# Two products of a 4-bit weight decode: one VectorE operation or two on GpSimd, in a kernel whose order of work is planned

## The chip, the cores and the metric

The kernel runs on one core of a Trainium2 chip. The metric is the device time of one execution in microseconds (us), the median of several. The engines of a core work side by side, each through its own queue of instructions in order: TensorE (PE in the profile, its weight loads PEld), VectorE (DVE), ScalarE (ACT), GpSimd (POOL) and SyncE (SP), which here only issues DMA transfers. An instruction waits on semaphores for what it needs, and everything behind it in its queue waits with it.

## The reference

A layer adds two branches to its input `x` of 8 sequences x 256 tokens x 256 features, both from the same normalized input.

- Attention branch, 16 heads of 128: `q`, `k`, `v` and a gate by weights of 256 x 2048; `q` and `k` are turned by position (rope). A low-rank product gives 64 states per head and token, `s`; `es = exp(s)` and `z` is the running log-sum-exp of `s` over the tokens. `ok = exp(-z) * (masked(q k^T) @ es)`, a softmax over the 64 states, then `W2 = masked((softmax * exp(-z)) @ es^T)`, `o = W2 @ v`, an RMS norm, the gate, and a product with `Wo`.
- Feed-forward branch of width 2048 whose three weight matrices are stored as 4-bit codes with one scale for each block of 32:

```python
idx = jnp.stack([W_packed & 15, W_packed >> 4 & 15], axis=-1).reshape(N, -1)
vals = NVFP4_LUT[idx]              # 0, 0.5, 1, 1.5, 2, 3, 4, 6 and their negatives
W = vals.reshape(N, K // 32, 32) * scales[:, :, None]
...
gelu = tanh(0.79788 * (gate + 0.044715 * gate ** 3)) * gate * 0.5 + gate * 0.5
out = (gelu * up) @ Wd.T
```

All of it is fp32.

## The kernel before

**Tiles.** The 2048 tokens are worked in 4 groups of 512. A step `n` is one group and one pair of heads: 4 x 8 = 32 steps, with a step -1 ahead that prepares step 0, and a last one that finishes. For a step, PE does `rope` four times (Q and K of two heads, L645), `states` (L584), `value` and `gate` (`vg`, L706), `scores` for each head (L725, L728), `logits` (L745), `cross` (L820), `weights` (L845, with `apply`, L872), `outputs` for each head (L888) and, every second step, `close` (L941), the product with `Wo`. Between these, units of the feed-forward branch are fed: `ffn_gate` (L437), `ffn_up` (L466) and `ffn_down` (L491): for each quarter of the width and each token group four gate and up pairs, then two down projections.

**Who does what around them.** For a rope, ScalarE copies the swapped halves of the PSUM result (`z`, L655 and L656), VectorE multiplies by the cosine (L658), and GpSimd multiplies `z` by the sine (L663) and adds (L664). The scores are masked by VectorE (L716). `states` is clipped (L598), turned to `u` and `es` by ScalarE and a transpose through DRAM (L602, L519, L523, L532, L612), summed along the tokens by a VectorE scan (L624) and inverted (L630). The softmax takes row maxima on VectorE (L781, L786) and exponentials on ScalarE (L792); GpSimd multiplies the result by `enz` (L803). `outputs` ends in a power on GpSimd (L910), for which VectorE's product (L914) waits. The norm of later groups is on VectorE (L290 to L306) and ScalarE (L309). A gate unit uses ScalarE, GpSimd (L446) and VectorE (L448, L452), an up unit VectorE (L475).

**The decode.** 24 parts (4 quarters, each with two halves of gate, up and down) are decoded into `w_gate`, `w_up` and `w_down` by `decode_next`. For one part VectorE shifts the codes so that a 4-bit code's fields land in sign, exponent and mantissa of an fp32 number (L388, twice), masks them (L392), and multiplies by a power of two and by the scales (L394). The buffer `u` has two copies and is shared with `states`; `pk` (codes) and `sc` (scales) have three, and SP loads the next when their last reader is done.

**The order.** Each engine's queue is written out by the program itself while it is built, and kept as written (`tc.manual_schedule()`). PE's units are placed at fractions of a step by the tables `POS`, `START`, `NORM_AT`, and feed-forward units are spread by `FEED`, `FIRST` and `LAST`; `DUE` says how many parts have been decoded by which step. The work of the other engines is written as chains: a generator yields an engine and an assumed cost ("v" VectorE, "s" ScalarE, "g" GpSimd, "d" DMA issue) ahead of each operation, and `advance` always writes out the chain that could begin first by assumed clocks (then by `rank`; the decode has the lowest). A changed cost or place so moves other operations in the queues, too.

Of the kernel before, what the change touches and what calls it, by code (L numbers as in the profile page):

```python
# [10 lines left out]
F32 = mybir.dt.float32  # L11
I32 = mybir.dt.int32
AF = mybir.ActivationFunctionType
ALU = mybir.AluOpType
# [3 lines left out]
P = 128  # L18
# [15 lines left out]


POS = {'scores': (0.054, 0.064),
 'logits': (0.12,),
 'softmax': (0.335,),
 'cross': (0.147,),
 'weights': (0.169,),  # L40
 'low': (0.121,),
 'states': (0.167,),
 'outputs': (0.364, 0.453),
 'close': (0.384, 0.559),
 'rope': (0.176, 0.315, 0.368, 0.485),
 'vg': (0.561, 0.79, 0.922, 0.953)}
START = {-1: {'states': (0.575,), 'rope': (0.155, 0.358, 0.421, 0.588)},
 0: {'vg': (0, 0.013, 0.059, 0.197),
     'scores': (0.082, 0.162),
     'states': (0.336,),  # L50
     'logits': (0.251,),
     'softmax': (0.433,),
     'rope': (0.211, 0.24, 0.245, 0.458)}}
FEED = {-1: (0.336, 1.0)}
NORMS = {0: 1, 2: 2, 5: 3}
WO = (1, 3, 4, 6)
NORM_AT = (0.204, 0.657)
FIRST = [0.27, 1.57]
LAST = [1.65, 3.53]
DUE = [4, 6, 7, 7, 9, 9, 10, 11, 11, 11, 12, 13, 14, 15, 16, 16, 16, 17, 18, 19, 19, 22, 23, 23, 24]  # L60


@with_exitstack
def layer_kernel(ctx: ExitStack, tc: tile.TileContext, a: dict, out: bass.AP):
# [15 lines left out]
    nc = tc.nc  # L80
# [84 lines left out]
    def new(pool, shape, tag, bufs=1, dtype=F32):  # L165

        users = held.setdefault(tag, [])
        if len(users) >= bufs:
            while any(c in chains for c in users[-bufs]):
                advance()  # L170
            floor[0] = max([floor[0]] + [c.at for c in users[-bufs]])
        t = pool.tile(shape, dtype, tag=tag, name=tag, bufs=bufs)
        users.append([])
        at_tag[id(t)] = t, users[-1]
        return t
# [8 lines left out]
    def chain(gen, *tiles, rank=1, at=0.0):  # L184


        c = Chain()
        c.rank = rank
        c.banks = []
        c.gen, c.at, c.what = gen, max(clock["pe"] + 0.2, floor[0], at), next(gen)  # L190
        floor[0] = 0.0
        chains.append(c)
        for t in tiles:
            users = at_tag[id(t)][1]
            users.append(c)
            if id(t) in banks_taken:
                c.banks.append(users)
        return c
# [155 lines left out]
    LD, CH = 512, 256  # L354
# [3 lines left out]
    def load_packed(m):  # L358

        if m < 12:  # L360
            pk = new(de, [P, LD], "pk", 3, I32)
            sc = new(de, [P, LD], "sc", 3)
            nc.sync.dma_start(out=pk, in_=a["codes"][m])
            nc.sync.dma_start(out=sc, in_=a["scales"][m])
            packed[m] = pk, sc
            loads(m, 512)

    def decode_next():

        q, k = divmod(len(parts), 6)
        m, o = 3 * q + (0, 1, 0, 1, 2, 2)[k], (0, 0, CH, CH, 0, CH)[k]
        if k == 1 and q:
            load_packed(m + 1)
        if k >= 4:
            load_packed(3 * q + k - 1)
        w = (w_gate, w_up, w_down)[m % 3]
        pks, scs = packed[m]
        pk, sc = pks[:, o : o + CH], scs[:, o : o + CH]  # L380
        f = q * LD + o if m % 3 == 2 else o // CH * (MLP // 2) + q * CH
        w = w[:, :, f : f + CH]
        u = new(de, [P, 2, CH], "u", 2, I32)

        def work():
            yield "v", 0.6
            for k, left in enumerate((28, 24)):
                nc.vector.tensor_scalar(  # L388
                    u[:, k, :], pk, left, 6, ALU.logical_shift_left, ALU.arith_shift_right
                )  # L390
            yield "v", 1.4
            nc.vector.tensor_scalar(u, u, 0x81C00000 - (1 << 32), None, ALU.bitwise_and)  # L392

            nc.vector.scalar_tensor_tensor(  # L394
                w, u.bitcast(F32), 2.0 ** (125 if m % 3 == 2 else 126),
                sc.unsqueeze(1).to_broadcast([P, 2, CH]), ALU.mult, ALU.mult,
            )

        parts.append(chain(work(), pks, scs, u, rank=2, at=landed[m]))

    inter = {}
# [96 lines left out]
    def ffn():  # L498

        for q in range(4):  # L500
            for g in range(NG):
                for n in blocks(q):
                    yield ffn_gate, g, n
                    yield ffn_up, g, n
                for i in (0, 2):
                    yield ffn_down, g, q, i
# [464 lines left out]
    banks = NG * (MLP // P * 2 + 8)  # L971
    weight = FIRST + [1.0] * (N + 2 - len(FIRST) - len(LAST)) + LAST
    feeding = list(ffn())
# [29 lines left out]
    for n in range(-1, N + 1):  # L1003
        at = []
        pos = START.get(n, {})

# [4 lines left out]
        def put_at(place, f, *args):  # L1011
            at.append((place, len(at), f, args))

        def put_norm(g, places):
            for k, h in enumerate((0, 2)):
                put_at(places[k], norm, g, h)
# [24 lines left out]
        if gn:  # L1041
            if gn > 1:
                put_at(0.0, load_x, gn * TC, TC)
            put_norm(gn, NORM_AT)
        if n > 0:
# [10 lines left out]
        upto = round(banks * sum(weight[: n + 2]) / sum(weight))  # L1056
        lo, hi = FEED.get(n, (0.0, 1.0))
        for k in range(upto - fed):
            put_at(lo + (hi - lo) * (k + 0.5) / (upto - fed), feed)
        fed = upto  # L1060
        upto = DUE[n + 1] if n + 1 < len(DUE) else 24
        for k in range(sent, upto):
# [93 lines left out]
```

## Time and profile before

| | |
|---|---|
| median of 3 runs | 1188.27 us (1187.34 to 1188.94) |
| the profiled execution, its own time | 1187.13 us |
| its span in the profile | 1185.3 us |
| granted TensorE clock | 1.00 |
| ScalarE busy | 536.3 us (45%) |
| DMA, mean | 114 GB/s |
| HBM read and written | 88.47 MB, 45.61 MB |

The span runs from the first instruction's start to the last one's end. "Busy" is the union of an engine's instructions; idle time is put down to what released the next instruction. PE's matmuls are pipelined and their ends modelled, so where PE lost time is read from the start of a matmul after a gap. Rows of groups have the form: line, engine, operation, out<-in, shapes, count | busy us, mean ns of one | idle us of the engine ahead of them, and what ended it. All lines in the text are those of the kernel before; in the changed kernel those after the decode stand 3 lower.

### The profile page before, as it was taken

How to read it: one execution, taken by the hardware profiler on the slowest of the kernel's cores; microseconds unless marked ns; L12 is line 12 of the kernel's file. 1: busy time of each engine (PE TensorE's matmuls, PEld its weight loads, DVE VectorE, ACT ScalarE, POOL GpSimd, SP SyncE). 2: the span in 40 equal slices, each digit the busy share in tenths (PEclk: the TensorE clock that was granted, in tenths of full speed). 3: DMA queues.
4: the chain of work that ended last, by engine and by line, in shares of the span. 5: the costliest groups of instructions: out<-in, count | busy, mean ns of one | idle time of the engine just before them, and what ended most of it. 6: DMA issues, size and time to landing. Idle time of an engine off the chain costs nothing.

```text
span 1185.3 us, 18158 instructions
## 1 busy us (share of the span) xinstructions
PE 1171.9 (99%) x5830; PEld 827.7 (70%) x5830; DVE 884.7 (75%) x1690; ACT 536.3 (45%) x1685; POOL 494.1 (42%) x439
## 2 busy tenths in 40 slices
PE   9899999999999999999999999999999999999998
PEld 6466776866767777667767677686776777766775
DVE  7978968887677788767587875968778577768553
ACT  3545535455344444443354543435544444445321
POOL 5434525554344444434344442434544334445110
PEclk9999999999999999999999999999999999999999
DMA  6335444453333342333344243434333333432321
GB/s 209 116 105 153 143 118 152 132 144 116 101 119 117 110 140 84 107 113 107 90 142 123 86 121 107 120 103 122 96 97 96 116 116 107 124 102 88 98 64 61
DMA packets 143087, 135.30 MB, mean 114 GB/s; under 512 B 21264, under 2 KB 110480, under 8 KB 142992
## 3 DMA queue, kind: packets, MB, share of 16 engines
q1 hardware_dynamic: 142992, 134.15, 38.5%
q8 instruction: 46, 0.75, 0.3%
q14 instruction: 49, 0.40, 0.1%
HBM read 88.47 MB, written 45.61 MB: 113 GB/s over the span
## 4 chain that ended last, share of the span: by engine, by line
PE 89%; DVE 6%; DMA 2%; issue 1%; POOL 1%; ACT 1%; SPq 1%; DVEq 0%; ACTq 0%; POOLq 0%
PE ps L645 17%; PE ps L706 17%; PE ps L491 9%; PE ps L941 9%; PE ps L437 8%; PE ps L466 8%; PE ps L888 5%; PE ps L725 4%; PE ps L745 3%; PE ps L845 3%; PE ps L728 2%; PE ps L584 2%; PE ps L872 1%; PE ps L820 1%; DVE enz L630 1%
## 5 line engine op out<-in xcount | busy, mean ns | idle before, releaser
L663 POOL TENSOR_TENSOR z<-z,turns 128x512 f32<-128x512 f32 x128 | 169.4, 1324 | 209.3 <-ACT z L656 209.0
L645 PE MATMUL ps<-xT,wts 128*128 128x512 f32 x512 | 239.2, 599 | 0.5 <-ACT xT L349 0.5
L706 PE MATMUL ps<-wts,xT 128*128 128x256 f32 x1024 | 235.7, 379 | 1.5 <-DVE og L914 1.1
L706 PEld LDWEIGHTS ps<-wts,xT 128*128 128x128 f32 x1024 | 194.4, 190 | 54.1 <-issue 24.4
L645 PEld LDWEIGHTS ps<-xT,wts 128*128 128x128 f32 x512 | 90.1, 190 | 82.0 <-issue 75.1
L446 POOL TENSOR_SCALAR t<-t 128x512 f32<-128x512 f32 x64 | 40.2, 629 | 196.6 <-ACT t L444 194.6
L437 PE MATMUL ps<-xT,w_gate 128*128 128x512 f32 x256 | 120.7, 594 | 0.1
L466 PE MATMUL ps<-xT,w_up 128*128 128x512 f32 x256 | 120.6, 594 | 0.0
L630 DVE RECIPROCAL enz<-enz 128x128 f32<-128x128 f32 x128 | 117.6, 932 | 0.0
L491 PE MATMUL ps<-w_down,inter 128*128 128x256 f32 x512 | 115.3, 380 | 0.0
L941 PE MATMUL ps<-w_o,ogT 128*128 128x256 f32 x496 | 112.1, 379 | 0.0
L941 PEld LDWEIGHTS ps<-w_o,ogT 128*128 128x128 f32 x496 | 94.1, 190 | 24.7 <-issue 12.4
L491 PEld LDWEIGHTS ps<-w_down,inter 128*128 128x128 f32 x512 | 96.6, 190 | 15.9 <-issue 3.2
L655 ACT COPY z<-ps 64x512 f32<-64x512 f32 x128 | 74.5, 582 | 69.8 <-PE ps L645 60.3
L444 ACT ACTIVATE t<-ps 128x512 f32<-128x512 f32 x64 | 38.2, 596 | 137.9 <-PE ps L437 137.8
L910 POOL TENSOR_TENSOR ss<-ss,nhalf 128x4 f32<-128x4 f32 x64 | 66.0, 1032 | 69.7 <-DVE ss L906 68.4
L409 DVE TENSOR_TENSOR res<-ps,res 128x512 f32<-128x512 f32 x63 | 42.9, 681 | 69.5 <-PE ps L491 48.0
L664 POOL TENSOR_TENSOR k<-k,z 128x512 f32<-128x512 f32 x64 | 83.7, 1308 | 26.5 <-DVE k L658 16.7
L664 POOL TENSOR_TENSOR q<-q,z 128x512 f32<-128x512 f32 x64 | 85.0, 1328 | 21.2 <-DVE q L658 17.2
L803 POOL TENSOR_TENSOR prT<-okT,enz 128x512 f32<-128x512 f32 x32 | 40.8, 1274 | 119.9 <-DMA okT<-by_way 106.6
L792 ACT ACTIVATE ok<-okT,mx 128x64 f32<-128x64 f32 x256 | 85.7, 339 | 10.8 <-DVE mx L786 10.3
L448 DVE TENSOR_TENSOR t<-ps,t 128x512 f32<-128x512 f32 x64 | 43.7, 684 | 60.9 <-POOL t L446 60.7
(83 smaller groups left out, 1936.6 us busy)
## 6 DMA issues: line engine op xcount, KB each, us to landing
wts<-in_wqkvg_dram SPq DMA_DIRECT2D x64, 512.0 KB, 3.8
by_way<-ok SPq DMA_DIRECT2D x256, 64.0 KB, 1.8
okT<-by_way SPq DMA_DIRECT2D x64, 256.0 KB, 2.7
by_way<-og SPq DMA_DIRECT2D x256, 64.0 KB, 1.8
ogT<-by_way SPq DMA_DIRECT2D x64, 256.0 KB, 2.9
by_way<-u SPq DMA_DIRECT2D x128, 64.0 KB, 1.8
u<-by_way SPq DMA_DIRECT2D x32, 256.0 KB, 2.8
pk<-in_codes_dram SPq DMA_DIRECT2D x12, 256.0 KB, 3.1
```

Source lines behind the costliest of these rows:

```text
L437: nc.tensor.matmul(pg, lhsT=w_gate[:, c, ns], rhs=xT[:, c, gs], start=c == 0, stop=c == 1)
L466: nc.tensor.matmul(pu, lhsT=w_up[:, c, ns], rhs=xT[:, c, gs], start=c == 0, stop=c == 1)
L491: nc.tensor.matmul(ps[:, k, :], lhsT=inter[g, n][0][:, (i + k) * P : (i + k + 1) * P], rhs=w_dn[:, n, :], start=n == 2 * q, stop=n == 2 * ...
L630: nc.vector.reciprocal(r, r)
L645: nc.tensor.matmul(ps, lhsT=w[:, c, :], rhs=xT[:, c, g * G : (g + 1) * G], start=c == 0, stop=c == 1)
L655: nc.scalar.copy(z[0:64], pv[64:128])
L663: nc.gpsimd.tensor_tensor(z, z, sin_b, ALU.mult)
L664: nc.gpsimd.tensor_tensor(y, y, z, ALU.add)
L706: nc.tensor.matmul(ps[:, k, :], lhsT=xT[:, c, tt], rhs=w[:, which, c, :], start=c == 0, stop=c == 1,)
L792: nc.scalar.activation(pr[:, js, i, :], okT[:, js, i, :], AF.Exp, bias=mx[:, k : k + 1], scale=SCALE, accum_out=sm[:, k : k + 1],)
L910: nc.gpsimd.tensor_tensor(ss, ss, nhalf, ALU.pow)
L941: nc.tensor.matmul(ps[:, k, :], lhsT=ogT[hh][0][:, i + k], rhs=w_o[:, (hp // 2) * 4 + hh, :], start=hh == 0, stop=hh == 3,)
```

## The change

The cost assumed for L392 is 0.5 us by itself; the two products become two GpSimd operations with an assumed cost of 1.95 us: first by the power of two, from `u` into the weight tile, then by the scales in place. The tables of places and the number of decoded parts by step are set anew.

```diff
 POS = {'scores': (0.054, 0.064),
- 'logits': (0.12,),
+ 'logits': (0.148,),
...
- 'low': (0.121,),
+ 'low': (0.116,),
...
- 'close': (0.384, 0.559),
- 'rope': (0.176, 0.315, 0.368, 0.485),
+ 'close': (0.372, 0.61),
+ 'rope': (0.176, 0.368, 0.375, 0.523),
...
-START = {-1: {'states': (0.575,), 'rope': (0.155, 0.358, 0.421, 0.588)},
- 0: {'vg': (0, 0.013, 0.059, 0.197),
+START = {-1: {'states': (0.575,), 'rope': (0.155, 0.358, 0.421, 0.592)},
+ 0: {'vg': (0.044, 0.057, 0.103, 0.241),
...
-     'rope': (0.211, 0.24, 0.245, 0.458)}}
-FEED = {-1: (0.336, 1.0)}
+     'rope': (0.238, 0.267, 0.272, 0.485)}}
+FEED = {-1: (0.443, 1.0)}
...
-NORM_AT = (0.204, 0.657)
-FIRST = [0.27, 1.57]
-LAST = [1.65, 3.53]
-DUE = [4, 6, 7, 7, 9, 9, 10, 11, 11, 11, 12, 13, 14, 15, 16, 16, 16, 17, 18, 19, 19, 22, 23, 23, 24]
+NORM_AT = (0.204, 0.593)
+FIRST = [0.17, 1.57]
+LAST = [1.56, 3.5]
+DUE = [4, 6, 7, 7, 8, 9, 11, 11, 11, 11, 12, 13, 14, 15, 16, 16, 16, 16, 18, 19, 19, 22, 23, 23, 24]
...
-            yield "v", 1.4
+            yield "v", 0.5
             nc.vector.tensor_scalar(u, u, 0x81C00000 - (1 << 32), None, ALU.bitwise_and)
-
-            nc.vector.scalar_tensor_tensor(
-                w, u.bitcast(F32), 2.0 ** (125 if m % 3 == 2 else 126),
-                sc.unsqueeze(1).to_broadcast([P, 2, CH]), ALU.mult, ALU.mult,
+            yield "g", 1.95
+
+            nc.gpsimd.tensor_scalar(
+                w, u.bitcast(F32), 2.0 ** (125 if m % 3 == 2 else 126), None, ALU.mult
+            )
+            nc.gpsimd.tensor_tensor(
+                w, w, sc.unsqueeze(1).to_broadcast([P, 2, CH]), ALU.mult
             )
```

## The prediction

> **What bounds the kernel now.** I read the busy times first, then a table of stretches, then who waited for whom before 62 us, and last the timeline where TensorE (PE) waits. Busy times:
>
> ```profile
> PE 1171.9 (99%) x5830; PEld 827.7 (70%) x5830; DVE 884.7 (75%) x1690; ACT 536.3 (45%) x1685; POOL 494.1 (42%) x439
> ```
>
> PE lacks 13.4 us in a span of 1185.3, and no change to other engines can give back more. Where they lie (stretch, then its length, then PE, PEld, DVE, ACT, POOL busy):
>
> ```profile
> 0.00:10.00 10.00, 7.90 (x40) 6.65 (x41) 3.98 (x15) 2.58 (x5) 3.07 (x13) 1.00 0.72 229
> 20.00:40.00 20.00, 19.12 (x74) 12.50 (x75) 19.75 (x34) 8.33 (x15) 10.21 (x9) 1.00 0.30 98
> 40.00:60.00 20.00, 16.05 (x67) 8.62 (x64) 19.72 (x43) 11.27 (x31) 10.47 (x10) 1.00 0.50 146
> 60.00:200.00 140.00, 138.20 (x682) 96.11 (x679) 114.04 (x218) 67.16 (x211) 64.46 (x57) 1.00 0.48 140
> 200.00:1100.00 900.00, 898.76 (x4562) 640.59 (x4560) 677.75 (x1291) 420.95 (x1343) 388.56 (x334) 1.00 0.38 111
> 1100.00:1186.00 86.00, 81.89 (x386) 58.97 (x384) 41.12 (x80) 20.64 (x71) 11.48 (x14) 1.00 0.23 72
> ```
>
> 2.1 us are lost before the first work and 4.1 at the end (0.7 of that is the table's 1186.0 against the span's 1185.3); nothing in the diff reaches the loads and the last output that cause most of these. Between 200 and 1100 us PE lacks 1.2 us in 900. What can move is 20 to 60 us, 4.8 us, where VectorE (DVE) is busy 39.5 of 40, and 60 to 200 us, 1.8. The operations that the edit touches or copies:
>
> ```profile
> L394 DVE SCALAR_TENSOR_TENSOR w_gate<-u,sc 128x512 f32<-128x512 f32 x8 | 8.7, 1083 | 0.3
> L394 DVE SCALAR_TENSOR_TENSOR w_up<-u,sc 128x512 f32<-128x512 f32 x8 | 7.4, 930 | 0.3
> L394 DVE SCALAR_TENSOR_TENSOR w_down<-u,sc 128x512 f32<-128x512 f32 x8 | 6.5, 811 | 0.3
> L446 POOL TENSOR_SCALAR t<-t 128x512 f32<-128x512 f32 x64 | 40.2, 629 | 196.6 <-ACT t L444 194.6 <-DVE eps L798 0.4
> L803 POOL TENSOR_TENSOR prT<-okT,enz 128x512 f32<-128x512 f32 x32 | 40.8, 1274 | 119.9 <-DMA okT<-by_way 106.6 <-PE ps L728 10.8 <-PE ps L820 2.3
> ```
>
> The longest PE stall of the run, in the timeline (start, length, engine, line):
>
> ```profile
> 51.03 0.58 ACT L655 COPY z<-ps 64x512 f32<-64x512 f32 x1
> 51.62 0.58 ACT L656 COPY z<-ps 64x512 f32<-64x512 f32 x1
> 52.63 0.62 ACT L309 ACTIVATE z<-res,off,rstd 128x256 f32<-128x256 f32 x1 [0.43 <-DVE off L306]
> 53.15 0.33 ACT L792 ACTIVATE ok<-okT,mx 128x64 f32<-128x64 f32 x1
> 53.23 1.27 POOL L663 TENSOR_TENSOR z<-z,turns 128x512 f32<-128x512 f32 x1
> 54.68 1.27 POOL L664 TENSOR_TENSOR k<-k,z 128x512 f32<-128x512 f32 x1 [0.18 <-DVE k L658]
> 56.01 0.70 PE L725 MATMUL ps<-q,k 128*128 128x256 f32 x2 [2.61 <-POOL k L664]
> ```
>
> The scores of step 1's second head need K, and K needs ScalarE's two copies (L655, L656), then two GpSimd products (L663, L664). The copies were done at 52.20, before the norm (L309) and the softmax exponentials (L792). Soon after, PE waits 1.34 and 0.19 us more for VectorE's L716; its first down projection (L491) starts at 61.79.
>
> **The change part by part.** *Removed:* 24 operations, 8 x 1083 + 8 x 930 + 8 x 811 = 22.6 us of VectorE. The shortest is 0.69 us, so 16.6 us are work and 6.0 are waiting: at 12.57 one took 1.64 while GpSimd's L663 ran from 12.36 to 13.66.
>
> *Added:* 24 x (0.63 by L446 + 1.27 by L803) = 45.6 us of GpSimd, 494 to 540 us, 46% of the span: no bound. [...] More GpSimd time also holds up VectorE's other two-SBUF operations; against 22.6 us of relief at 75% load I cost this at nothing after 60 us. Cover gone, it is the 6.0 us above scaled by 45.6/494, 0.6 us.
>
> *Moved, up to 60 us.* START and FEED only change the sequence of PE's first units, not their number: at 37 us both orders have done the same ones. I read the built order of each queue and laid rows of the same shape along it. Six of the 24 decodes lie here. On GpSimd the first now stands ahead of the first rope: 12.6 + 0.63 + 1.27 = 14.5, where L663 started at 12.36. The second stands between the third and fourth rope, ready about 25.8, while the first up projection is reached at 24.5: PE waits 1.3. In exchange the two waits of before at 29.24 and 30.65 (0.40 and 0.48 idle) shrink, since VectorE loses six products of 1.64, 1.64, 0.98, 0.69, 0.69 and 0.69 = 6.3 us. PE is then some 1 us late, which the next stall swallows.
>
> *That stall grows.* rope's new places (0.368, 0.375, 0.523 for 0.315, 0.368, 0.485) and the planner's new costs put ScalarE's two copies for this K behind both norm operations, all eight exponentials and the copy of es (L612). In the old trace that group runs from 52.63 to 56.91, 4.3 us. It can't start before the row maxima (L786). Logits come earlier, about 37 for 39.4, but on VectorE the maxima now stand behind two scans (L624) and a K product, which meet GpSimd at two decodes on end. I take the start as 53.15, as before, give or take 1. Copies then run from 57.4 to 58.6, the two GpSimd products to 61.2; L725 starts at 61.2 (60.2 to 62.2) for 56.01, 5.2 later. Behind K's product on VectorE, ahead of the last L716, stand L658, two L452, two L475, L392 and two L716: 0.68 + 1.36 + 1.38 + 0.43 + 1.1 = 5.0 from 58.6 to 63.6. PE, after scores (1.3) and cross (0.5), is ready at 63.0: 0.6 idle for 1.53. Net at the first down projection: 5.2 - 0.9 = +4.3, with bounds +2.4 and +5.9.
>
> *After 62 us.* 18 decodes remain, 1.9 us of GpSimd each. In seven the next GpSimd instruction is the power L910, for which VectorE's L914 waits, with all behind it. Bounds: -1.8 (all idle between 60 and 200 us gone; logits moved from 0.12 to 0.148 give L716 1 us more) and 7 x 1.9 = +13.3 (nothing hidden). The nearest row is the 1.2 us that PE lacks in 900 us with GpSimd 43% busy, so near the lower end: +1.0. The decodes end about 850 us; the last step's order on PE is the same, so the end (FIRST, LAST, close) costs nothing; without that cover, a wait like the 0.33 us of L888 at 1145.71. Norms, DUE and SP: the load of the third scales waits on SP for GpSimd's product (about 32 us) instead of VectorE's (24.1), with the next weights behind it; those are needed near 75 us, so nothing.
>
> *Sum.* The profiled execution took 1187.13, 1.83 above its span, and 1.14 under the median. 1187.13 + 4.3 + 1.0 = 1192.4; with 1.1 to the median, 1193.5. Bounds: 1188.3 + 2.4 - 1.8 = 1188.9 and 1188.3 + 5.9 + 4 = 1198.2 (4: two of the seven places unhidden).
>
> **The rivals.** *Faster (0.16).* VectorE is what PE waits for until 60 us; it loses 6.3 us there, the exponentials start early enough (before 49 us) for the copies to be no later than before, and the idle time of 0.40, 0.48, 1.34, 0.19 and 2.61 goes: 5.0 us, 1183.3. For it: DVE's 39.5 of 40. Against: the order on ScalarE. It decides if K's copies end before 52.2.
>
> *No change (0.14).* PE stays at 99% with all of it hidden: K late by 2 us, the later waits less by 2: 1188.3. For it: 1.2 us idle in 900.
>
> *GpSimd's queue becomes the chain after 62 us (0.12).* More than two of the seven powers reach PE: 4.3 + 13.3, 1205.9 at most, about 1202. Against it: VectorE's idle quarter.
>
> That the change does less than it says is excluded: all 24 pairs stand in GpSimd's built order.
>
> **How the numbers follow.** Forecast 0.58 (1188.9 to 1198.2). With 0.12 for the third rival, whose time is above the forecast, slower by over 0.2% has 0.70; 0.2% (2.4 us) is about what a measurement of this kernel can tell from no change. The range, 1185.0 to 1201.0, leaves out most of the fast case and the top of the third rival.
>
> **What the profile would show.** Right: L394 gone, 24 pairs on POOL of 0.63 and 1.3 us; VectorE near 860 us; the longest PE stall before L725 near 55 to 61 us, put to GpSimd's K, with ScalarE's copies directly after L612; first L491 near 66. Wrong: that L725 starts by 57 us, PE idle before 60 us under 5 us, or PE idle between 200 and 1100 us over 5.

## The result, and the profile after

The change makes the kernel slower by 0.3%: 1191.79 us (1189.97 to 1193.48, 9 runs) against 1187.69 us (1187.15 to 1188.94, 9 runs) of the kernel before on the same chip, a ratio of 1.0029 with an interval of 1.0020 to 1.0038. That is 4.1 us, where 5.3 were forecast. The profiled execution took 1191.79 us, with a span of 1189.6, 4.3 us more than before. Busy times after:

```profile
PE 1173.1 (99%) x5830; PEld 828.9 (70%) x5830; DVE 872.0 (73%) x1666; ACT 537.7 (45%) x1685; POOL 557.1 (47%) x487
```

VectorE lost 12.7 us and GpSimd gained 63.0; the forecast had 22.6 and 45.6. The table of stretches (start and end, length, then PE, PEld, DVE, ACT, POOL, the granted clock, DMA share, GB/s) shows where PE stands still now:

```profile
20.00:40.00 20.00, 18.44 (x81) 12.45 (x80) 19.44 (x34) 8.53 (x16) 15.79 (x14) 1.00 0.35 106
40.00:60.00 20.00, 14.16 (x40) 6.44 (x38) 17.16 (x38) 11.48 (x31) 14.05 (x13) 0.92 0.47 134
60.00:200.00 140.00, 137.94 (x686) 97.97 (x687) 109.61 (x215) 65.99 (x209) 75.84 (x66) 0.97 0.49 135
200.00:1100.00 900.00, 899.38 (x4561) 639.18 (x4560) 674.19 (x1277) 422.24 (x1343) 428.02 (x363) 1.00 0.39 112
```

From 20 to 60 us PE lacks 1.56 + 5.84 = 7.4 us where it lacked 4.8. In the 900 us after 200 it lacks 0.6, half of what it lacked before. The clock column is new: it is below 1.00 in two rows. The timeline around the longest stall (start, length, engine, line; what ended the wait in brackets):

```profile
51.88 0.35 ACT L795 ACTIVATE ok<-okT,mx 128x64 f32<-128x64 f32 x1 [0.37 <-DMA wts<-in_wqkvg_dram]
...
56.43 0.60 ACT L615 COPY es<-u 128x512 f32<-128x512 f32 x1
...
57.06 0.58 ACT L658 COPY z<-ps 64x512 f32<-64x512 f32 x1
57.66 0.58 ACT L659 COPY z<-ps 64x512 f32<-64x512 f32 x1
...
58.74 1.27 POOL L666 TENSOR_TENSOR z<-z,turns 128x512 f32<-128x512 f32 x1 [3.48 <-ACT z L659]
...
60.19 1.27 POOL L667 TENSOR_TENSOR k<-k,z 128x512 f32<-128x512 f32 x1 [0.18 <-DVE k L661]
...
61.51 1.22 PE L728 MATMUL ps<-q,k 128*128 128x256 f32 x2 [6.73 <-POOL k L667]
```

ScalarE's copies for K stand directly behind the copy of `es`, and the scores start at 61.51 us. The first of these products took 1.22 us; the same one took 0.70 at 53.21. Four windows of the same table, a few microseconds long, show the granted clock at that time (the third number from the right):

```profile
54.00:58.00 4.00, 0.79 (x6) 0.54 (x4) 4.00 (x10) 3.88 (x13) 1.17 (x2) 0.87 0.01 3
58.00:62.00 4.00, 0.49 (x1) 0.49 (x2) 4.00 (x9) 1.38 (x3) 2.54 (x2) 0.50 0.30 80
...
64.00:66.00 2.00, 2.00 (x15) 1.53 (x15) 0.56 (x1) 0.37 (x1) 1.92 (x3) 0.50 0.67 180
66.00:68.00 2.00, 2.00 (x16) 1.40 (x13) 0.26 (x1) 0.00 (x0) 0.92 (x1) 0.71 0.37 80
```

While PE stood still its granted clock fell to 0.50. It was back at 1.00 only at about 67.2 us (a mean of 0.71 over 2 us is 1.2 us at a half), 5.7 us after work resumed. If a half clock does half the work, an estimate (the product above took 1.22 us for 0.70), those 5.7 us cost 2.8.

At the end of the run PE waits once more, for the last softmax but one (`prT`):

```profile
1112.75 1.16 PE L848 MATMUL ps<-prT,esT 64*128 64x128 f32 x16 [1.23 <-POOL prT L806]
```

The last group that matters is that of the new products:

```profile
L395 POOL TENSOR_SCALAR w_up<-u 128x512 f32<-128x512 f32 x8 | 12.8, 1601 | 11.5 <-DVE u L392 11.0 <-DVE eps L801 0.4
...
L395 POOL TENSOR_SCALAR w_gate<-u 128x512 f32<-128x512 f32 x8 | 12.0, 1497 | 6.1 <-DVE u L392 4.9 <-DVE ss L909 1.1
...
L398 POOL TENSOR_TENSOR w_down<-w_down,sc 128x512 f32<-128x512 f32 x8 | 10.2, 1274 | 0.7
...
L449 POOL TENSOR_SCALAR t<-t 128x512 f32<-128x512 f32 x64 | 40.0, 624 | 143.6 <-ACT t L447 140.9
```

The second product (L398) costs the 1.27 us that L803 had shown. The first (L395) costs 1.5 to 1.6 us, where L449, an operation of the same kind, shape and engine, costs 0.62.

### The profile page after: what moved, and what is told of

Read it like the earlier page. It is cut to its first block, busy times and chain, and to the rows that moved or that the text cites. A ratio compares the mean times of both kernels' runs of the same rounds, so it can differ in the third digit from the quotient of the medians.

```text
span 1189.6 us, 18152 instructions
## 1 busy us (share of the span) xinstructions
PE 1173.1 (99%) x5830; PEld 828.9 (70%) x5830; DVE 872.0 (73%) x1666; ACT 537.7 (45%) x1685; POOL 557.1 (47%) x487
## 4 chain that ended last, share of the span: by engine, by line
PE 91%; POOL 3%; DMA 2%; DVE 2%; issue 1%; ACT 1%; SPq 0%; POOLq 0%; DVEq 0%; ACTq 0%
PE ps L648 18%; PE ps L709 17%; PE ps L944 9%; PE ps L494 9%; PE ps L440 8%; PE ps L469 8%; PE ps L891 5%; PE ps L728 4%; PE ps L748 3%; PE ps L848 2%; PE ps L731 2%; PE ps L587 2%; PE ps L823 2%; PE ps L875 1%; DMA okT<-by_way 1%
## 5 line engine op out<-in xcount | busy, mean ns | idle before, releaser
L449 POOL TENSOR_SCALAR t<-t 128x512 f32<-128x512 f32 x64 | 40.0, 624 | 143.6 <-ACT t L447 140.9
L891 PEld LDWEIGHTS ps<-v,wt 128*128 128x128 f32 x512 | 66.0, 191 | 28.6 <-issue 13.9
L728 PE MATMUL ps<-q,k 128*128 128x256 f32 x256 | 77.7, 385 | 7.7 <-POOL k L667 7.7
```

What stands on the lines that cost most here:

```text
L728: nc.tensor.matmul(ps[:, 0:T], lhsT=k[:, b, 0:P], rhs=q[:, b, :], start=True, stop=True)
L891: nc.tensor.matmul(po[:, i, :], lhsT=wt[:, i, :], rhs=v[:, i, j * DK : (j + 1) * DK], start=False, stop=i == TC - 1,)
```

## The experiments

Two theories at the start. *A:* the new order costs the time, through the stall at K. *B:* the operation costs it, because its GpSimd time holds somebody up. Unless said otherwise each edit is against the changed kernel, times are medians, and the ratio is to the kernel before, measured beside it (1187.7 to 1188.1 us). Times inside a profile are those of one execution; executions of one kernel lie 1 to 7 us apart, so differences of under a microsecond between two profiles are a hint only.

**The order alone** (`e1_order_only`): the new tables and assumed costs, with VectorE's one operation where the pair stood.

```diff
-            nc.gpsimd.tensor_scalar(
-                w, u.bitcast(F32), 2.0 ** (125 if m % 3 == 2 else 126), None, ALU.mult
-            )
-            nc.gpsimd.tensor_tensor(
-                w, w, sc.unsqueeze(1).to_broadcast([P, 2, CH]), ALU.mult
+            nc.vector.scalar_tensor_tensor(
+                w, u.bitcast(F32), 2.0 ** (125 if m % 3 == 2 else 126),
+                sc.unsqueeze(1).to_broadcast([P, 2, CH]), ALU.mult, ALU.mult,
             )
```

> The changed kernel's queues on every engine as they are, but each decode's products are again one VectorE operation, where its pair of GpSimd operations stood in the order. Theory A (the new order costs the time: on ScalarE the two copies for K of step 1's second head stand behind the softmax exponentials): the scores of that head still start at 60 to 62 us, the first down projection at 65.5 to 68 (67.62 in the changed kernel, 61.79 before), and the time is 1190 to 1192. Theory B (the GpSimd operations cost it: 1.5 and 1.27 us each ahead of the ropes): the scores start by 57, the first down projection by 63, and the time is 1187 to 1188.5.

1188.35 us, 1.0002 (0.9993 to 1.0011). The stall is there all the same: the scores of the second head wait 6.6 us and start at 60.56, and the first down projection starts at 65.85, as A expected; the time is the one that B expected. The end of the span comes 0.2 us after that of before. Starts of the same units in three profiles, with the delay to before:

| start of | before | after | order alone |
|---|---|---|---|
| first down projection | 61.79 | 67.62 (+5.83) | 65.85 (+4.06) |
| scores, step 4 | 163.71 | 167.15 (+3.44) | 164.92 (+1.21) |
| scores, step 8 | 300.94 | 304.75 (+3.81) | 301.94 (+1.00) |
| scores, step 28 | 1000.41 | 1002.98 (+2.57) | 1000.24 (-0.17) |
| scores, step 31 | 1100.21 | 1102.38 (+2.17) | 1099.64 (-0.57) |
| end of the span | 1185.35 | 1189.64 (+4.29) | 1185.59 (+0.24) |

The new order loses 4 us at K and has it back by the end: waits that before had after 62 us, such as 1.06 us at 119.63 and 0.40 at 128.66, are gone. From 60 to 1100 us PE lacks 1.3 us here and 3.0 before; the difference is less than half of what comes back, and where the rest lies was not found. (Feed-forward units that moved between steps are part of the single rows, not of the last one.) Theory A falls. What is left, 4.05 us of span, is the operation in this order: 1.8 by the first down projection, 1.0 more by step 28, 1.3 in the last steps. Of the 1.8, 0.95 is K's later arrival (scores at 61.51 for 60.56) and 0.8 is, by the estimate above, a longer time at half clock after it (5.7 us for 4.0).

**The operation alone** (`e2_op_only`): the tables and assumed costs of before, with the GpSimd pair.

```diff
-            nc.vector.scalar_tensor_tensor(
-                w, u.bitcast(F32), 2.0 ** (125 if m % 3 == 2 else 126),
-                sc.unsqueeze(1).to_broadcast([P, 2, CH]), ALU.mult, ALU.mult,
+            nc.gpsimd.tensor_scalar(
+                w, u.bitcast(F32), 2.0 ** (125 if m % 3 == 2 else 126), None, ALU.mult
+            )
+            nc.gpsimd.tensor_tensor(
+                w, w, sc.unsqueeze(1).to_broadcast([P, 2, CH]), ALU.mult
             )
```

(against the kernel before)

> The kernel before with its places, its assumed costs and so its queues, only that each decode's single VectorE product is the pair of GpSimd operations. Theory A: the scores of step 1's second head start within 1.5 us of 56.0, the first down projection within 2 of 61.79, no down-clocking, and the time is 1187 to 1189.5, the small loss from the first gate or up projection that waits for its weights. Theory B: 1191 or more, with the first down projection later than 65.

1206.8 us, 1.0156 (1.0142 to 1.0170). In the list of waits (for whom; total us, times, longest) K's GpSimd product leads:

```profile
PE ps L727 <- POOL k L666: 14.6, 5, 5.9
```

Without new places the operation costs 18.7 us; the tables take back 15 of them. So one part of the change is a repair of the other.

**K's copies first** (`e3_copies_first`): the chain of step 1's ropes is written out ahead of others that could begin at the same time.

```diff
-        first = chain(work(), ps, y, z)
+        first = chain(work(), ps, y, z, rank=-1 if n == 1 else 1)
```

> The changed kernel with one more word: the chain that copies rope's results on ScalarE has the first rank in the planner for step 1, so that the copies for K of the second head stand ahead of the exponentials. Theory A: those copies start near 51.5 us instead of 57.06, the scores at 55 to 57 instead of 61.51, the granted clock stays at 1.00 between 40 and 70 us, the first down projection starts at 61 to 63.5, and 4 to 6 us of the run go: 1185.5 to 1188. Theory B: the scores stay at 60 or later and the time within 1 us of 1191.8.

1195.79 us, 1.0060 (1.0047 to 1.0074): a miss. The copies went only to 54.50, still behind a gate's activation that waits for PE, and the scores to 59.98. But a down projection moved behind the product that needs `prT`, which now waits 5.3 us, and the first down projection starts at 75.03. One rank moves operations of other chains, too, so this run tells nothing on the stall itself.

**The stall filled** (`e4_fill`): PE multiplies ones into the bank of the scores that it waits to compute, so that it is not idle; nothing else moves.

```diff
             ps = bank()
+            for _ in range(28 if (n, j, b) == (1, 1, 0) else 0):
+                nc.tensor.matmul(ps[:, 0:P], lhsT=ones, rhs=ones, start=True, stop=True)
```

> The changed kernel with 28 matmuls of ones, 128x128, ahead of the scores of step 1's second head, about 6.1 us of work in the 6.73 us in which PE waits; their result is overwritten. It tells what the granted clock of 0.50 between 58 and 66 us costs by itself. If the clock falls because PE stands still (theory C): it stays at 1.00, the scores still start at 61.5, but the first down projection comes at 65.2 to 66 instead of 67.62, and the time falls by 1.5 to 2.5 us, to 1189.3 to 1190.3. If the clock is not what makes the 6.1 us between scores and down projection (a wait on VectorE's L719 instead): no change, 1191.8 within 0.5.

1191.26 us, 1.0021 (1.0010 to 1.0032): the clock and the down projection do what theory C expected, the time doesn't. The clock stays up:

```profile
58.00:62.00 4.00, 3.53 (x31) 3.34 (x30) 4.00 (x11) 1.62 (x3) 2.55 (x2) 1.00 0.25 68
...
64.00:66.00 2.00, 1.85 (x19) 1.06 (x15) 0.72 (x2) 0.32 (x1) 1.92 (x3) 1.00 0.60 166
```

The scores start at 61.74, no earlier than without the fill, and the first down projection at 65.13, 2.5 us earlier: that is the price of the half clock at this place, near the 2.8 estimated above. PE stays 2.1 to 3.4 us ahead in the steps looked at up to step 31, and then loses it:

```profile
1111.09 2.08 PE L850 MATMUL ps<-prT,esT 64*128 64x128 f32 x16 [2.62 <-POOL prT L808]
```

The clock falls here, too: it stands at 0.50 for 3.4 us from 1110.7, of which PE works 3.0; by the same estimate that costs another 1.5. The span ends 0.3 us before that of the changed kernel. So a microsecond that is won anywhere must also pass this place.

**The form of the first product** (`e5_forms`): three forms, one for each of the weights. The gate's has two operations; the up one writes in place on `u`; for the down one VectorE also sets exponent bits (the first lines of the cut, in place of L392), so that no number is tiny. The down weights are other numbers then, so only the lengths of the operations count in this run.

```diff
+            if m % 3 == 2:
+                nc.vector.tensor_scalar(
+                    u, u, 0x81C00000 - (1 << 32), 0x3F800000, ALU.bitwise_and, ALU.bitwise_or
+                )
...
+            if m % 3 == 0:
+                nc.gpsimd.tensor_scalar(w, u.bitcast(F32), p2, 1.0, ALU.mult, ALU.mult)
...
+            elif m % 3 == 1:
+                uf = u.bitcast(F32)
+                nc.gpsimd.tensor_scalar(uf, uf, p2, None, ALU.mult)
...
+            else:
+                nc.gpsimd.tensor_scalar(w, u.bitcast(F32), 0.5, None, ALU.mult)
```

> The question is why the first product on GpSimd (L395) takes 1.5 us where L449, a product and a sum over the same 128x512 numbers, takes 0.63. The gate's decodes keep the numbers and use two operations in one instruction (times 1); the up ones keep one operation but write in place; the down ones get exponent bits set so that no number is below the smallest normal one (the decoded down weights are other numbers then). Theory 'one operation': the gate's form falls to 0.63, the others stay near 1.5. Theory 'another tile': the up form falls to 0.63. Theory 'the numbers' (codes masked to a sign, two exponent bits and one bit of fraction, many of them below the normal range): the down form falls to 0.63, the others stay. If all stay near 1.5, it is contention with VectorE. Time within 1188 to 1194.

```profile
L406 POOL TENSOR_SCALAR u<-u 128x512 f32<-128x512 f32 x8 | 12.8, 1606 | 11.5 <-DMA wts<-in_wqkvg_dram 9.1 <-DVE u L397 2.0 <-DVE eps L811 0.4
...
L409 POOL TENSOR_SCALAR w_down<-u 128x512 f32<-128x512 f32 x8 | 12.4, 1544 | 3.5 <-DVE u L393 2.5 <-DVE eps L811 0.9
...
L402 POOL TENSOR_SCALAR w_gate<-u 128x512 f32<-128x512 f32 x8 | 5.0, 620 | 6.4 <-DVE u L397 5.2 <-DVE ss L919 1.1
```

One execution took 1190.06 us. Only the gate's row fell, to 620 ns. It is neither the numbers nor the tile: on these 128x512 tiles a `tensor_scalar` with one operation takes 1.5 to 1.6 us on GpSimd, and with a second one that multiplies by 1 it takes 0.62, where VectorE's one product took 0.69 at the least in the kernel before.

**Which decodes** (`e7_first_v` and `e8_first_g`): the first six on VectorE and the later eighteen on GpSimd, and the other way round (`q > 0` for `q == 0`).

```diff
+            if q == 0:
+                nc.vector.scalar_tensor_tensor(
...
+            else:
+                nc.gpsimd.tensor_scalar(
...
+                nc.gpsimd.tensor_tensor(
```

> The first six products on VectorE in one operation, the later eighteen on GpSimd as after the change; orders of TensorE, ScalarE and SP as after. Theory 'start' (the operation costs through the six early decodes, while VectorE and GpSimd are both full): near the order alone, 1188.3 to 1189.5, first down projection near 65.9 us. Theory 'later' (it costs through eighteen decodes spread over 60 to 850 us, which meet the powers and VectorE's operations): 1190.5 to 1192, although the first down projection is at 65.9. If the time goes up only at the last steps, where no decode lies, it is the chain of the last steps that gives away what came before.

> The complement: the first six products on GpSimd, the later eighteen in one VectorE operation. Theory 'start': 1190.5 to 1192, first down projection near 67.6 us. Theory 'later': 1188.3 to 1189.5, though the first down projection is at 67.6.

With the first six on VectorE: 1188.17 us, 1.0003 (0.9994 to 1.0012), the same as the order alone. With the first six on GpSimd: 1189.71, 1.0016 (1.0007 to 1.0025). The eighteen later decodes alone cost nothing that can be measured; the six early ones alone cost 1.4 us against the order alone, about half of the operation's cost. All 24 together cost 2.1 us more than the six by the medians, so the two parts don't add up; the intervals of these two ratios overlap. In the profiles 0.5 of that is there at the first down projection, 1.0 more by step 8, and 0.9 comes in the last steps. The 0.5 is the clock: the scores start at 61.47 and 61.51 after waits of 6.72 and 6.73 us, and full clock is back at 66.2 with the six and at 67.2 with all 24. The 0.9 is the wait for `prT`: 1.23 us with all 24, 0.30 with the six, 0.34 with the eighteen. What makes the 1.0, and that wait longer with all 24, was not found.

**K early by its place** (`e9_rope_start`): the first places of rope and the feed of before.

```diff
-     'rope': (0.238, 0.267, 0.272, 0.485)}}
-FEED = {-1: (0.443, 1.0)}
+     'rope': (0.211, 0.24, 0.245, 0.458)}}
+FEED = {-1: (0.336, 1.0)}
```

> After, with rope's first places and the feed of before (START's rope from 0.211, FEED 0.336): in the built order ScalarE's two copies for K of step 1's second head stand ahead of the exponentials again, and a gate unit stands one place later on TensorE. Theory 'that stall is the loss': the scores wait under 3 us, the clock stays up, first down projection by 64 us, time 1187 to 1189. Theory 'a stall before 62 us is regained or replaced later' (as the order alone suggested): the stall goes and the time stays at 1190 to 1194.

1199.02 us, 1.0089 (1.0075 to 1.0103), worse than both expectations. The stall at K is nearly halved, and another has come:

```profile
PE ps L848 <- POOL prT L806: 9.8, 4, 8.1
...
PE ps L728 <- POOL k L667: 3.7, 2, 3.4
```

The copies now stand ahead of the exponentials, these start at 61.20 instead of 51.88, and `prT` with them: PE waits 8.1 us for it at 73.16. ScalarE's place for K and for the softmax is one place; the long stall at K is the cheaper choice in this order.

**The cheap form** (`e10_two_ops`), **with the fill** (`e11_two_ops_fill`), **and in the old order** (`e12_old_order`):

```diff
             nc.gpsimd.tensor_scalar(
-                w, u.bitcast(F32), 2.0 ** (125 if m % 3 == 2 else 126), None, ALU.mult
+                w, u.bitcast(F32), 2.0 ** (125 if m % 3 == 2 else 126), 1.0,
+                ALU.mult, ALU.mult,
             )
```

> After, with a second operation (times 1.0) in the first GpSimd product, the form that took 0.62 us in the run of the forms where the plain one takes 1.5. Order as after. Theory 'the operation's slowness at the start is the loss': the first up projection's wait falls from 1.6 to under 0.4, first down projection near 65.5 us, GpSimd 557 minus 24 x 0.9 = about 535 us, time 1188 to 1189.5. Theory 'the second product or the place is the loss, the first one's length is hidden': first down at 67 or later, 1190.5 to 1192.

> The same, with the 28 products of ones that keep TensorE at work in the wait for K. Theory 'the clock's fall after the stall costs 2 us or more, and the cheap form takes the rest': clock 1.00 in 60 to 70 us, first down near 63.5 us, time 1186 to 1188, that is at or below before. Theory 'the last steps give it back' (SP's transfers ahead of the last softmax's, then prT): the first down as early, a wait of 2 us or more for prT near 1107 us, time within 0.5 us of the run without the fill.

> The order and costs of before, with the GpSimd pair in the cheap form; with the plain form this order took 1206.8. If the slow form is most of that loss of 18.7 us: 1194 or less, and TensorE's waits for K (14.6 us) fall under 6. If it is that K's products stand behind any decode on GpSimd's queue, whatever its form: 1200 to 1206.

The cheap form: 1189.91 us, 1.0014 (1.0005 to 1.0023), GpSimd 535.4 us. The first up projection waits 0.56 us instead of 1.56, the first down projection starts at 66.85, and the span is 2.6 us shorter. It lies between the two expectations: the form is about half of the loss.

In the old order: 1195.43 us, 1.0059 (1.0045 to 1.0073), so 11.4 of the 18.7 us were the slow form. The time is a little above the 1194 expected, and the waits for K are still 9.5 us, above the 6 expected, where the kernel before has 3.0. That K's products stand behind decodes in GpSimd's queue fits this, but it was not tried by itself.

With the fill as well: 1189.14 us, 1.0002 (0.9993 to 1.0011), no difference from before. The first down projection starts at 64.29, step 31's scores at 1097.27, 3.3 us earlier than without the fill, and the span ends at the same 1187.0. So each expectation held in part: the first at the start of the kernel, the second in its last steps. The queue of DMA issues (SPq) there:

```profile
1095.88 2.83 SPq L527 DMA_DIRECT2D by_way<-og  x4
1098.75 0.43 SPq L258 DMA_DIRECT2D wts<-in_wqkvg_dram  x1
1099.29 1.84 SPq L527 DMA_DIRECT2D by_way<-ok  x4
1101.24 0.41 SPq L536 DMA_DIRECT2D ogT<-by_way  x1
1103.62 0.34 SPq L536 DMA_DIRECT2D okT<-by_way  x1
```

VectorE had transposed `ok` by 1095.2, but its transfers stand behind those of `og` and a load of weights, so that `okT` is asked for at 1103.62, `prT` starts at 1107.21, and PE waits 2.1 us for it. The clock falls with this wait as well (windows as above):

```profile
1108.00:1110.00 2.00, 1.47 (x16) 1.48 (x18) 0.00 (x0) 0.00 (x0) 0.47 (x1) 0.74 0.76 228
1110.00:1112.00 2.00, 2.00 (x14) 1.64 (x11) 1.29 (x2) 0.00 (x0) 0.00 (x0) 0.50 0.13 34
```

It stands at 0.50 for 3.4 us, nearly all of them work, which by the estimate above costs some 1.7 more. Not every execution shows it: five of the eleven have a mean clock of 1.00 and took 1185.9 to 1187.9 us, six have 0.999 and took 1189.1 to 1190.9.

**The last steps** (`e13_last_steps`), on top of the cheap form and the fill:

```diff
-        to["ogT", j] = ogT, chain(after(), og, ogT)
+        to["ogT", j] = ogT, chain(after(), og, ogT, rank=2 if n == N - 3 else 1)
...
-            put("vg", 3, load_w, n + 1, 2)
+            if n != N - 2:
+                put("vg", 3, load_w, n + 1, 2)
+            if n == N - 1:
+                put_at(0.06, load_w, n, 2)
```

> The cheap form and the fill, and in the last steps SP issues the last softmax's transposed probabilities ahead of the weights of step 31 and without waiting for ogT's landing in between; half a down projection moves ahead of the product that needs prT. Theory 'the last steps gave the gain back, by SP's order': the wait of 2.3 us for prT falls under 0.5, the end comes 2 us or more before the run without this edit, 1186 to 1187.5, so at or below before. Theory 'another input comes last there' (SP's first issue of the second group again takes over a microsecond, or the weights of step 31 come late): a wait of the same size at another line, 1188.5 to 1190.

1185.38 us (1185.01 to 1186.23, 11 runs), 0.9980 (0.9971 to 0.9989): faster than both kernels, by 2.4 us than the one before and by some 6 than the changed one. The wait for `prT` near 1110 us is gone, and the mean clock is 1.00 in all 11 executions:

```profile
1098.61 1.83 SPq L527 DMA_DIRECT2D by_way<-ok  x4
...
1102.06 0.32 SPq L536 DMA_DIRECT2D okT<-by_way  x1
```

`okT` is asked for 1.6 us earlier, and the down projection is whole ahead of L851. SP's order is here the one of the kernel before again: all of `og`, then `ok`, then the load of weights and the reads. In the two profiles the stretch from step 31's scores to the end of the span is 89.7 us without this edit and 86.0 with it: 3.7 less, about what the 2.1 of wait and the estimated 1.7 of half clock come to. The parts of this edit were not tried apart. Nor were the fill and this edit tried with the products on VectorE, so this run doesn't say that GpSimd is the better place for them.

## Why the prediction was right or wrong, point by point

The forecast case came: a slower kernel, with a longer stall at K, at 1191.79 us for the forecast 1193.5. But that is partly luck: errors cancelled, in the sum and inside its terms, and the stall that the forecast put the loss on does not by itself cost the time, as the order alone shows.

- *Removed from VectorE.* The 22.6 us of L394 are gone, VectorE fell by 12.7 and not to near 860. Other rows grew: the shifts (L388) from 18.1 to 25.0 us, 23.3 in the order alone, and `ss` (L906, now L909) from 20.2 to 33.2, 32.1 in the order alone; others shrank. All of VectorE's rows but the products add up (rows overlap, so the sum is above the busy time) to 937.7 us before, 941.0 in the order alone and 947.9 after, so a third of what came back is the order's and the rest came with the operation. The prediction costed GpSimd's hold on VectorE at nothing after 60 us. In the trace of before some of VectorE's operations took longer beside GpSimd's: on average the scan (L624) took 0.66 us where no GpSimd operation ran beside it and 1.10 where one did for over 30% of its time, `ss` (L906) 0.13 and 0.53, and the masks (L392), with one input, 0.42 and 0.81. The reciprocals (L630) took 0.93 either way.
- *Added to GpSimd.* This term was mis-sized: the six rows of L395 and L398 add up to 67.9 us, not 45.6 (GpSimd's total rose by 63.0, as its other rows fell by some 5). The second product was right. The first was taken from L446, which has two operations; the new one has one. The nearest row by kind and shape was the wrong row, and no row of before has the form of L395.
- *The first up projection.* Forecast 1.3 us of wait, measured 1.56. With the cheap form, whose length the forecast had assumed, it is 0.56: the forecast was 0.7 too high, and the slow form hid that.
- *The stall at K.* Right in its cause and place: copies behind the exponentials and the copy of `es`, forecast for 57.4, measured 57.06; the scores forecast for 61.2, measured 61.51. The times agree by luck: ScalarE's group started at 51.88 and not at 53.15, and took 5.2 us and not 4.3, of which it waited 0.77 for the norm's `off`. That the places of rope were the cause was named too narrowly: giving back its first places brings the copies forward and moves the softmax back by more.
- *The first down projection.* Forecast +4.3 (2.4 to 5.9), measured +5.83. The step that failed is "scores (1.3) and cross (0.5)" at the lengths of the rows of before: after the stall PE ran at half clock, and the fill shows 2.5 us for it. The old stall of 2.6 us had left the clock at 1.00 in the profiled execution, so the trace of before gave no sign. Half clock (0.50) lasted 10.24 us here, 6.83 in the order alone and 3.41 in the last steps with the fill. It also came with a wait of 2.1 us, in the last steps with the cheap form and the fill. In other executions of the kernel before the clock does not stay up either: of the 21 measured beside the cheap form, five have a mean clock of 0.997 and took 1188.6 to 1190.8 us, the others 0.999 or more and 1186.8 to 1188.5.
- *After 62 us.* Forecast +1.0. From the first down projection to step 31 the delay went from 5.83 to 2.17, so -3.7. The order alone gave 4.6 us back there, and the operation took 1.0. The bound of -1.8 counted PE's idle time between 60 and 200 us only. This term, "near the lower end: +1.0", was wrong by 4.7 us, the largest error of the sum.
- *The end.* "The end costs nothing" failed: the delay grows by 2.1 us after step 31's scores, 0.8 of it in the order alone, and PE waits 1.23 us for `prT`. As far as the traces show, the price came through SP's queue: `okT` was asked for 5.1 us after VectorE had transposed `ok` before, and 7.7 after the change, as a load of weights and a read of `ogT` now stand ahead of `ok`. The order alone has the same 7.7 and no such wait, though, and what makes its 0.8 was not found.
- *The sum.* 4.3 + 1.0 + 0 was forecast; 5.8 - 3.7 + 2.1 = 4.3 us of span was measured, with the rounding.
- *The rivals.* "Faster" needed K's copies to end before 52.2 us; they ended at 58.2. "No change" needed the later waits to shrink by what K is late; the order alone does just that, and the operation takes it away. The third rival, the chain through the powers, did not come: PE lacks 0.6 us between 200 and 1100 us.

## What to carry to other kernels

A term taken from the nearest row needs the same form of instruction, not only the same kind and shape: how many operations it holds belongs to the form (here 1.5 us with one, 0.62 with two). Where a stall of several microseconds is forecast, look in a profile for what such a stall does to the clock (here 0.50 with a wait of 6.73 us), and count the work after it at that clock. In a kernel with an order written out by a planner, ask of each microsecond won or lost whether it reaches the end: here a loss of 4 us at 60 us was regained by 1000, and a gain of 3 was lost at 1110 until the transfers ahead of the last softmax but one were moved, with half a down projection that moved too.

## What the runs showed of the hardware that was not expected

- GpSimd's `tensor_scalar` on 128x512 fp32: 1.50 us with one multiplication, 0.62 us with two (the second by 1.0), on the same data and tiles (the rows of `w_gate` after the change and in the run of the forms).
- In the 14 traces the granted TensorE clock fell 17 times ahead of the end of the run. It stood at 0.50 for 3.41 us (seven times), 6.83 (seven) or 10.24 (three: after the change, with the cheap form, and with K early by its place). Each of the 12 PE waits of 3.1 us or more came with such a fall, and none of those under 2.0. In between it fell with waits of 2.0 us (K early by its place), 2.12 (the cheap form with the fill), 2.62 (the fill) and 2.72 (K's copies first) and not with the one of 2.61 in the kernel before, so there the length of the wait doesn't decide it.
- One of SP's four transfer issues of `og` in a row took 1.4 us with the cheap form and the fill, and 1.9 with the fill alone, where its neighbours take 0.4. What it waited for is not in the profile.
